# Attention weights of the last layer: block-diagonal tiles against dense tiles in pairs of 64 rows

## Chip, cores and metric

The kernel runs on one NeuronCore of a Trainium2 chip, in one launch. All data is float32. The metric is device time in microseconds (us). Three runs of the kernel before gave 1648.38, 1644.84 and 1645.3 us; the median is 1645.3 us.

## The reference, cut to what matters

128 sequences of 64 tokens with 128 channels go through four layers. Layers 0 to 2 are transformer blocks with 16 heads; the change does not touch what they compute. In layer 3 each sequence has a single-head attention over its own 64 context rows:

```
nx = layer_norm(x) * gamma + beta
q, k, v = nx @ Wq, ctx @ Wk, ctx @ Wv
weights = softmax(q k^T / sqrt(128))        # 64 x 64 for each sequence
evidence = weights @ v
combined = [nx, evidence, anchor]           # anchor: one vector per sequence
routed = sum over 3 experts of softmax(combined @ router_W) * (silu(combined @ e_w1) @ e_w2 + e_b2)
g = sigmoid(silu(combined @ gate_w1) @ gate_w2)
out = x + g * (routed @ out_w + out_b)
```

The kernel folds Wk into Wq, and Wv into the weights that evidence is multiplied by, so "evidence" in the kernel is softmax weights times raw context rows, called u.

## The kernel before, in words

The 8192 tokens are worked on in 16 groups (NST) of 512 tokens. A group is 8 sequences, held as four tiles (TT) of 128 rows, two sequences to a tile. Layers 0 to 2 alternate attention stages and MLP stages over the 16 groups. Layer 3 is the last stage, and it overlaps the end of the second MLP stage.

The order of every engine is written out by hand: pieces of work (small functions) are called one after the other, and each engine runs its instructions in the order of those calls. For layer 3 the list is `turn` (L1080): one turn does the hidden layers, the gate and the output of group a, and between them the attention pieces of groups a+1 and a+2. Turns 0 to 14 each hold one `turn_weights` and one `evidence`, for groups 1 to 15. Those of group 0 are called from `heads` (L1064), between the last turns of the MLP stage (L1199 to L1201); there `evidence` of group 0 follows directly on a `leave` of the MLP (L683: four transposes into the tile psB, which DVE then adds to x, L687).

The pieces that matter here, for one group:

- `load` (L897): one DMA from SP brings the context, tile c, 128 rows by 4 tiles by 128 channels (three buffers). `norm` (L903) loads the transposed context and lets POOL normalise x.
- `score` (L922): eight products of 64 columns give the scores psc (128 rows, 4 tiles, 64 keys), two sequences to a tile in the two halves of the rows. DVE subtracts the maximum.
- `weights` (L933): ACT takes the exponential, DVE the sum and its reciprocal. POOL then writes the shares into a tile pd of 128 rows by 4 tiles by 128 columns, in two instructions of 64 rows each (L943): sequence 0 of a tile into rows and columns 0 to 63, sequence 1 into rows and columns 64 to 127. The other half of pd is zero, set once by two memsets in `l3_loads` (L766).
- `turn_weights` (L947): four transposes of 128x128 (in the helper `transposed`, L317, so their line is L321) put pd's transpose into PSUM, and ACT copies 128x512 to pT (L950).
- `evidence` (L952): four products, context tile (128x128) as the stationary operand and 128 columns of pT as the moving one (L955). The zeros keep the two sequences apart. ACT copies 128x512 to u (L959).
- `router` (L961) and, in the next turn, `hidden` (L1005; L1013 and L1014) read u.

A float32 product is two instruction pairs on TensorE (a weight load and a matmul each); a transpose is one. So the four products of `evidence` are eight matmul records in the trace.

PSUM tiles of nx, queries, score, turn_weights, evidence and gate all come from the pool "mm" (L160), which has two buffers that are handed out in turn; a new tile waits for the readers of the tile that had its buffer.

Of the kernel before, what the change touches and what calls it, by code (L numbers as in the profile page):

```python
# [11 lines left out]
ALU = mybir.AluOpType  # L12
# [3 lines left out]
P = 128  # L16
NST = 16
TT = 4
NB = 8
L = 64  # L20
NT = TT * P
# [38 lines left out]
def tile_kernel(ctx: ExitStack, tc: tile.TileContext, a: dict, out: bass.AP):  # L60
    nc = tc.nc
    V, S, G, T = nc.vector, nc.scalar, nc.gpsimd, nc.tensor
# [3 lines left out]
    def const(shape, name):  # L66
        return cp.tile(shape, F32, tag=name, name=name)

    x_d = a["x"].rearrange("b n c -> (b n) c").rearrange("(s t p) c -> s p t c", t=TT, p=P)
    ctx_d = a["ctx_1024"].rearrange("b n c -> (b n) c").rearrange("(s t p) c -> s p t c", t=TT, p=P)  # L70
    out_d = out.rearrange("b n c -> (b n) c").rearrange("(s t p) c -> s p t c", t=TT, p=P)


# [32 lines left out]
    for name, n in (("L0_xcond_ca_proj_b", P), ("L1_xcond_bp", P), ("L2_xcond_b_cproj", P), ("L3_xcond_router_b", 3)):  # L106
        t = const([P, n], name)
# [10 lines left out]
    ident = const([P, P], "ident")  # L118
# [41 lines left out]
    def mm(name):  # L160
        return pools[1].tile([P, 512], F32, tag="mm", name=name)
# [150 lines left out]
    def stats_of(pool, src, eps):  # L312
        mv = pool.tile([P, TT, 2], F32, tag="mv", name="mv")
        stats(pool, src, mv)
        return mv, inv_std(pool, mv, eps)

    def transposed(psum, src):  # L317

        ps = psum.tile([P, 512], F32, tag="mm", name="psT")
        for t in range(TT):  # L320
            T.transpose(ps[:, ts(t, P)], src[:, t, :], ident)  # L321
        return ps
# [403 lines left out]
    def kept(shape, name, tag=None):  # L726
        return cp.tile(shape, F32, tag=tag or name, name=name)

    k3 = {}
    l3_pool = [None]  # L730

    def l3_loads():
        pool = l3_pool[0]
        e_w1 = a["L3_xcond_e_w1"].rearrange("e (k p) n -> p e k n", p=P)
        k3["w_1"] = kept([P, 3, 256], "w_1", "L0_xcond_adaln_w")
        k3["raw1"] = pool.tile([P, 6, 256], F32, tag="raw1", name="raw1", bufs=1)
        for ex in range(3):
            nc.sync.dma_start(k3["raw1"][:, 2 * ex : 2 * ex + 2], e_w1[:, ex, 1:3])
        k3["raw2"] = pool.tile([P, 6, P], F32, tag="raw2", name="raw2", bufs=1)
        nc.sync.dma_start(  # L740
            k3["raw2"], a["L3_xcond_e_w2"].rearrange("e (k p) n -> p (e k) n", p=P)
        )
        for ex in range(3):
            nc.sync.dma_start(k3["w_1"][:, ex], e_w1[:, ex, 0])
        r = _ROW["L3_xcond_gate_b2"]
        k3["g_b2"] = kept([P, P], "g_b2")
        nc.sync.dma_start(k3["g_b2"], a["vecs"][r : r + 1, :].broadcast_to([P, P]))
        r = _ROW["L3_xcond_out_b"]
        k3["out_b"] = kept([1, P], "out_b")
        nc.sync.dma_start(k3["out_b"], a["vecs"][r : r + 1, :])  # L750

        k3["r_b"] = kept([P, 1], "r_b")
        G.memset(k3["r_b"], 0.0)
        for t in range(TT):
            nc.sync.dma_start(
                k3["r_b"][32 * t : 32 * t + 3, :],
                a["L3_xcond_router_b"].rearrange("(n o) -> n o", o=1),
            )
        k3["one"] = kept([1, P], "one")
        G.memset(k3["one"], 1.0)  # L760
        k3["rw"] = kept([P, 3, 32], "rw")
        G.memset(k3["rw"], 0.0)
        k3["b_2o"] = kept([P, 3, P], "b_2o", "L0_xcond_fc1_w")
        for i in range(2):
            k3[f"pd{i}"] = kept([P, TT, P], f"pd{i}", ("L0_xcond_fc2_w", "L0_xcond_qkv_w")[i])
            G.memset(k3[f"pd{i}"], 0.0)  # L766
            k3[f"pr{i}"] = kept([P, TT, 3], f"pr{i}")
        k3["w_qk"] = kept([P, P], "w_qk")
        k3["w_gev"] = kept([P, P], "w_gev")
        k3["w_ev"] = kept([P, 3, 256], "w_ev", "L2_xcond_W_mod")  # L770
        k3["w_2o"] = kept([P, 6, P], "w_2o", "mod_L0_xcond_adaln_w")
        k3["ab"] = kept([P, 7, P], "ab")
        k3["ra"] = kept([P, NST, 2], "ra")
# [110 lines left out]
    def layer_3():  # L884

        pmm = pools[1]
# [6 lines left out]
        def sb(shape, tag, bufs=2):  # L893
            of = pools[0] if tag in shared else l3_pool[0]
            return of.tile(shape, F32, tag=shared.get(tag, tag), name=tag, bufs=bufs)

        def load(d):  # L897
            s = d["s"]
            d["c"] = sb([P, TT, P], "c", 3)
            nc.sync.dma_start(d["c"], ctx_d[s])  # L900
            d["mv"], d["rs"] = stats_of(l3_pool[0], xs[s], 1e-5)

        def norm(d):  # L903
# [29 lines left out]
        def weights(d):  # L933
            e = d["e"]
            S.activation(e, e, AF.Exp, scale=P ** -0.5)
            sm = sb([P, TT], "sm")
            V.tensor_reduce(sm, e, AX.X, ALU.add)
            V.reciprocal(sm, sm)

            pd = d["pd"] = k3["pd%d" % (d["s"] % 2)]  # L940
            for h in range(2):
                r = ts(h, L)
                G.tensor_tensor(  # L943
                    pd[r, :, r], e[r], sm[r].unsqueeze(2).broadcast_to([L, TT, L]), ALU.mult
                )

        def turn_weights(d):  # L947
            ps = transposed(pmm, d["pd"])
            d["pT"] = sb([P, NT], "pT")
            S.copy(d["pT"], ps)  # L950

        def evidence(d):  # L952
            ps = mm("pu")
            for t in range(TT):
                T.matmul(  # L955
                    ps[:, ts(t, P)], d["c"][:, t, :], d["pT"][:, ts(t, P)], start=True, stop=True
                )
            d["u"] = sb([P, NT], "u", 3)
            S.copy(d["u"], ps)  # L959

        def router(d):  # L961
            ps = small("pr")
# [97 lines left out]
        def go(f, j, *more):  # L1060
            if 0 <= j < NST:
                f(ds[j], *more)

        heads = [  # L1064
            lambda: (go(load, 0), go(load, 1)),
            lambda: go(norm, 0),
            lambda: (go(nx, 0), go(norm, 1)),
            lambda: (go(queries, 0), go(score, 0), go(load, 2)),
            lambda: (go(weights, 0), go(nx, 1), go(norm, 2)),
            lambda: (go(turn_weights, 0), go(queries, 1), go(score, 1)),  # L1070
            lambda: (go(evidence, 0), go(load, 3)),
        ]

        def bridge():
            go(router, 0)
            go(weights, 1)
            go(logits, 0)
            go(shares, 0)

        def turn(a_):  # L1080
            b_, c_ = a_ + 1, a_ + 2
            return [
                lambda: go(norm, c_ + 1),
                lambda: go(hidden, a_, 6),
                lambda: go(output, a_ - 1, 1),
                lambda: go(hidden, a_, 0),
                lambda: go(nx, c_),
                lambda: go(output, a_ - 1, 2),
                lambda: go(hidden, a_, 1),
                lambda: go(turn_weights, b_),  # L1090
                lambda: go(output, a_ - 1, 3),
                lambda: go(hidden, a_, 2),
                lambda: go(evidence, b_),
                lambda: go(load, c_ + 2),
                lambda: go(hidden, a_, 3),
                lambda: go(router, b_),
                lambda: go(hidden, a_, 4),
                lambda: go(biases, a_),
                lambda: go(queries, c_),
                lambda: go(hidden, a_, 5),  # L1100
                lambda: go(logits, b_),
                lambda: go(score, c_),
                lambda: go(gate, a_),
                lambda: go(output, a_, 0),
                lambda: go(shares, b_),
                lambda: go(weights, c_),
            ]
# [138 lines left out]
```

## Time and profile before

| | us |
|---|---|
| median of three runs | 1645.3 |
| profiled execution, own time | 1650.16 |
| its span, first to last instruction | 1648.4 |
| TensorE matmul (PE) busy over the span | 1590.4 |
| VectorE (DVE) busy | 1289.0 |
| GpSimd (POOL) busy | 1070.9 |
| ScalarE (ACT) busy | 1030.8 |
| TensorE clock granted, share of full | 0.996 |

The profile is of one execution. Its timeline lists instructions by start, with neighbours of one kind merged: start, duration, engine, line, operation, output<-inputs, for TensorE the part of the array used (rows*columns), the shape, and a count. The duration of a merged entry reaches to the end of its last instruction; since matmuls are pipelined, the next entry starts before that. PEld is the weight load that goes ahead of each matmul. A matmul's own duration holds the time it takes through the array, so the pace of the engine is read from start to start.

### The profile page before, as it was taken

How to read it: one execution, taken by the hardware profiler on the slowest of the kernel's cores; microseconds unless marked ns; L12 is line 12 of the kernel's file. 1: busy time of each engine (PE TensorE's matmuls, PEld its weight loads, DVE VectorE, ACT ScalarE, POOL GpSimd, SP SyncE). 2: the span in 40 equal slices, each digit the busy share in tenths (PEclk: the TensorE clock that was granted, in tenths of full speed). 3: DMA queues.
4: the chain of work that ended last, by engine and by line, in shares of the span. 5: the costliest groups of instructions: out<-in, count | busy, mean ns of one | idle time of the engine just before them, and what ended most of it. 6: DMA issues, size and time to landing. Idle time of an engine off the chain costs nothing.

```text
span 1648.4 us, 64206 instructions
## 1 busy us (share of the span) xinstructions
PE 1590.4 (96%) x27552; PEld 1066.6 (65%) x27552; DVE 1289.0 (78%) x2424; ACT 1030.8 (63%) x1696; POOL 1070.9 (65%) x1818
## 2 busy tenths in 40 slices
PE   6999999998999899999999999998999999999998
PEld 4677767776554467777776677776554566666665
DVE  6999989998576688899999999996453666666665
ACT  5878767776333677878878888885334444444442
POOL 5687777776899889987787776766654333334322
PEclk9999999999999999999999999999999999999999
DMA  7333443322202022212333432221200111111100
GB/s 206 81 93 86 105 119 91 89 79 61 60 27 60 21 60 62 66 47 55 86 94 85 107 85 73 62 60 43 79 1 7 35 34 36 39 33 39 30 14 17
DMA packets 137148, 104.15 MB, mean 63 GB/s; under 512 B 35045, under 2 KB 115615, under 8 KB 136863
## 3 DMA queue, kind: packets, MB, share of 16 engines
q1 hardware_dynamic: 136656, 100.01, 22.8%
q8 instruction: 217, 3.56, 0.9%
q14 instruction: 68, 0.56, 0.1%
q10 hardware_dynamic: 207, 0.03, 0.0%
HBM read 75.60 MB, written 13.89 MB: 54 GB/s over the span
## 4 chain that ended last, share of the span: by engine, by line
PE 78%; DVE 12%; ACT 3%; POOL 3%; DMA 2%; issue 2%; SPq 0%; POOLq 0%; DVEq 0%; ACTq 0%
PE sc L457 9%; PE pp L482 9%; PE po L499 7%; PE ph L1013 6%; PE ph L668 6%; PE ph L1014 6%; PE py L674 6%; PE psT L321 5%; PE po L1044 5%; DVE e L466 5%; DVE mx L464 5%; PE pk L415 4%; PE py L547 4%; PE pvv L438 3%; PE pq L428 3%
## 5 line engine op out<-in xcount | busy, mean ns | idle before, releaser
L486 ACT ACTIVATE eT<-pp 128x1024 f32<-128x1024 f32 x320 | 329.8, 1031 | 161.9 <-PE pp L482 161.9
L464 DVE TENSOR_REDUCE mx<-sc 128x32 f32<-128x2048 f32 x160 | 366.5, 2291 | 62.0 <-PE sc L457 62.0
L466 DVE TENSOR_TENSOR e<-sc,mx 128x2048 f32<-128x2048 f32 x160 | 366.6, 2291 | 5.5
L482 PEld LDWEIGHTS pp<-ident,e 64*128 64x128 f32 x5120 | 185.2, 140 | 142.4 <-ACT eT L486 45.2
L423 POOL TENSOR_SCALAR kbd<-kT,mask 128x512 f32<-128x512 f32 x316 | 213.2, 693 | 41.8 <-ACT kT L417 39.2
L482 PE MATMUL pp<-ident,e 64*128 64x64 f32 x5120 | 229.1, 230 | 8.4 <-DVE e L466 4.7
L351 POOL TENSOR_SCALAR xn<-x,nmu,rs 128x128 f32<-128x128 f32 x508 | 221.8, 451 | 13.3
L541 POOL TENSOR_TENSOR oT<-o,rb 128x512 f32<-128x512 f32 x80 | 102.1, 1276 | 154.3 <-DMA rb<-recs 71.3
L457 PE MATMUL sc<-kbd,qT 32*64 32x256 f32 x5120 | 181.0, 390 | 15.7 <-DVE e L466 14.6
L669 ACT ACTIVATE h<-ph,vec 128x512 f32<-128x512 f32 x128 | 87.4, 688 | 158.4 <-PE ph L668 158.3
L499 PE MATMUL po<-eT,vbd 128*32 128x64 f32 x10240 | 179.9, 222 | 1.6 <-issue 1.4
L1020 ACT ACTIVATE h<-h 128x512 f32<-128x512 f32 x112 | 69.1, 628 | 160.4 <-DVE h L1016 132.6
L499 PEld LDWEIGHTS po<-eT,vbd 128*32 128x32 f32 x10240 | 152.7, 110 | 15.1 <-issue 2.5
L309 POOL TENSOR_TENSOR rs<-rs,nhalf 128x4 f32<-128x4 f32 x128 | 130.4, 1018 | 10.7
L457 PEld LDWEIGHTS sc<-kbd,qT 32*64 32x64 f32 x5120 | 97.9, 132 | 52.8 <-issue 19.5
L1016 DVE TENSOR_TENSOR h<-ph,ab 128x512 f32<-128x512 f32 x112 | 76.9, 687 | 64.5 <-PE ph L1014 64.3
L299 DVE BATCH_NORM_STATS2 st<-x 128x6 f32<-128x128 f32 x512 | 110.4, 278 | 1.4 <-DMA x<-in_x_dram 0.8
L1037 POOL TENSOR_SCALAR g<-g 128x512 f32<-128x512 f32 x16 | 10.0, 625 | 140.4 <-ACT g L1036 140.4
L1013 PE MATMUL ph<-nx,w 128*128 128x512 f32 x192 | 99.8, 601 | 0.0
L507 ACT COPY o<-po 128x512 f32<-128x512 f32 x160 | 95.8, 598 | 5.8 <-PE po L499 3.3
L1044 PEld LDWEIGHTS po<-w_2o,h 128*128 128x128 f32 x768 | 92.2, 192 | 10.9 <-issue 8.4
L1049 DVE SCALAR_TENSOR_TENSOR acc<-po,pr,acc 128x128 f32<-128x128 f32 x192 | 67.2, 350 | 40.1 <-PE po L1044 35.6
(256 smaller groups left out, 2904.9 us busy)
## 6 DMA issues: line engine op xcount, KB each, us to landing
rb<-recs SPq DMA_DIRECT2D x80, 256.0 KB
c<-in_ctx_dram SPq DMA_DIRECT2D x80, 256.0 KB
o<-o SPq DMA_DIRECT2D x320, 32.0 KB
gt<-gate_L_xcond_sa_proj_w SPq DMA_DIRECT2D x32, 256.0 KB
gt<-gate_L_xcond_W_proj SPq DMA_DIRECT2D x32, 256.0 KB
x<-in_x_dram SPq DMA_DIRECT2D x16, 256.0 KB
ctxT<-cm SPq DMA_DIRECT2D x16, 256.0 KB
cT<-ctxT SPq DMA_DIRECT2D x16, 256.0 KB
```

The source lines that it names most:

```text
L299: V.bn_stats(st[:, t, :], src[:, t, :])
L309: G.tensor_tensor(rs, rs, nhalf, ALU.pow)
L351: engine.tensor_scalar(xn[:, t, :], src[:, t, :], nmu[:, t : t + 1], rs[:, t : t + 1], ALU.add, ALU.mult)
L423: (V if at.get("first") else G).tensor_scalar(kbd[:, j], by_batch(kT), mask[:, j : j + 1], 1.0, ALU.mult, ALU.mult)
L457: T.matmul(sc[ts(h, L), g, ts(t2, 256)], qT[ts(g, 32), ts(b, L)], kbd[ts(g, 32), :, b, :], start=True, stop=True,)
L464: V.tensor_reduce(mx, sc.rearrange("p g (m k) -> p (g m) k", k=L), AX.X, ALU.max)
L466: V.tensor_tensor(e, sc.rearrange("p g (m k) -> p (g m) k", k=L), mx.unsqueeze(2).broadcast_to([P, 32, L]), ALU.subtract,)
L482: T.transpose(pp[:, h, ts(4 * g2 + 2 * i + t2, L)], e6[ts(h, L), 2 * gg + g2, t2, i], ident[ts(h, L), ts(h, L)],)
L486: S.activation(eT[:, gg], pp, AF.Exp, scale=HD ** -0.5)
L499: T.matmul(po[ts(g, 32), i, ts(2 * t2 + h, L)], at["vbd"][:, 4 * u + 2 * t2 + h, 2 * g + i, :], e7[:, g // 2, h, g % 2, i, t2, :], start=T ...
L1013: T.matmul(ps, wn, d["nx"], start=True, stop=False)
L1044: T.matmul(po[:, ex, :], d[q][:, ts(t, P)], k3["w_2o"][:, q, :], start=r == 0, stop=r == 1)
```

## The change

The diff keeps the softmax shares dense. POOL writes one tile pn of 128 rows by 4 tiles by 64 keys in one instruction, and the zero-filled tiles and their memsets go. `turn_weights` transposes two tiles of 64 keys side by side as one 128x128 transpose, so there are two transposes for a group, and ACT copies 128x256. In the transpose, rows 0 to 63 hold the keys of the first tile of a pair and rows 64 to 127 those of the second (r = 0, 1); the columns hold the two sequences of a tile (h = 0, 1). `evidence` becomes eight products of 64 rows, 64x128 stationary and 64 columns moving, r = 0 and r = 1 in turn, on the upper and lower half of the array's rows. The two halves write to two PSUM tiles of the pool mm, and two ACT copies of 128x2x128 put them in order into u. The context is loaded to suit, with four DMAs of 64 rows by 2 sequences by 128 channels in place of one.

```diff
+    ctx_pairs = a["ctx_1024"].rearrange("(s i r h) k c -> s i r k h c", i=2, r=2, h=2)
...
         for i in range(2):
-            k3[f"pd{i}"] = kept([P, TT, P], f"pd{i}", ("L0_xcond_fc2_w", "L0_xcond_qkv_w")[i])
-            G.memset(k3[f"pd{i}"], 0.0)
             k3[f"pr{i}"] = kept([P, TT, 3], f"pr{i}")
...
         def load(d):
             s = d["s"]
-            d["c"] = sb([P, TT, P], "c", 3)
-            nc.sync.dma_start(d["c"], ctx_d[s])
+            d["c"] = sb([P, 4, P], "c", 3)
+            for i in range(2):
+                for r in range(2):
+                    nc.sync.dma_start(d["c"][ts(r, L), ts(i, 2), :], ctx_pairs[s, i, r])
...
-            pd = d["pd"] = k3["pd%d" % (d["s"] % 2)]
-            for h in range(2):
-                r = ts(h, L)
-                G.tensor_tensor(
-                    pd[r, :, r], e[r], sm[r].unsqueeze(2).broadcast_to([L, TT, L]), ALU.mult
+            d["pn"] = sb([P, TT, L], "pn")
+            G.tensor_tensor(
+                d["pn"], e, sm.unsqueeze(2).broadcast_to([P, TT, L]), ALU.mult
+            )
...
         def turn_weights(d):
-            ps = transposed(pmm, d["pd"])
-            d["pT"] = sb([P, NT], "pT")
-            S.copy(d["pT"], ps)
+            ps = mm("psT")
+            for i in range(2):
+                T.transpose(
+                    ps[:, ts(i, P)], d["pn"][:, ts(i, 2), :].rearrange("p t k -> p (t k)"), ident
                 )
+            d["pT"] = sb([P, 2, 2, L], "pT")
+            S.copy(d["pT"].rearrange("p i h q -> p (i h q)"), ps[:, 0 : 2 * P])
...
         def evidence(d):
-            ps = mm("pu")
-            for t in range(TT):
-                T.matmul(
-                    ps[:, ts(t, P)], d["c"][:, t, :], d["pT"][:, ts(t, P)], start=True, stop=True
-                )
+            ps = [mm("pu") for r in range(2)]
+            for i in range(2):
+                for h in range(2):
+                    for r in range(2):
+                        T.matmul(
+                            ps[r][:, ts(2 * i + h, L)], d["c"][ts(r, L), 2 * i + h, :],
+                            d["pT"][ts(r, L), i, h, :], start=True, stop=True,
+                        )
             d["u"] = sb([P, NT], "u", 3)
-            S.copy(d["u"], ps)
+            u4 = d["u"].rearrange("p (i r c) -> p r i c", i=2, r=2)
+            for r in range(2):
+                S.copy(u4[:, r], ps[r][:, 0 : 2 * P].rearrange("p (i c) -> p i c", i=2))
```

More of the change, by code (lines that the diff above doesn't have):

```diff
@@ L938, in weights, with turn_weights @@
             V.reciprocal(sm, sm)
-            pd = d["pd"] = k3["pd%d" % (d["s"] % 2)]
-            for h in range(2):
-                r = ts(h, L)
-                G.tensor_tensor(
-                    pd[r, :, r], e[r], sm[r].unsqueeze(2).broadcast_to([L, TT, L]), ALU.mult
-                )
-        def turn_weights(d):
-            ps = transposed(pmm, d["pd"])
-            d["pT"] = sb([P, NT], "pT")
-            S.copy(d["pT"], ps)
+            d["pn"] = sb([P, TT, L], "pn")
+            G.tensor_tensor(
+                d["pn"], e, sm.unsqueeze(2).broadcast_to([P, TT, L]), ALU.mult
+            )
+        def turn_weights(d):
+            ps = mm("psT")
+            for i in range(2):
+                T.transpose(
+                    ps[:, ts(i, P)], d["pn"][:, ts(i, 2), :].rearrange("p t k -> p (t k)"), ident
+                )
+            d["pT"] = sb([P, 2, 2, L], "pT")
+            S.copy(d["pT"].rearrange("p i h q -> p (i h q)"), ps[:, 0 : 2 * P])
         def evidence(d):
-            ps = mm("pu")
-            for t in range(TT):
-                T.matmul(
-                    ps[:, ts(t, P)], d["c"][:, t, :], d["pT"][:, ts(t, P)], start=True, stop=True
-                )
+            ps = [mm("pu") for r in range(2)]
[6 more added lines that the diff above has]
+                        )
             d["u"] = sb([P, NT], "u", 3)
-            S.copy(d["u"], ps)
+            u4 = d["u"].rearrange("p (i r c) -> p r i c", i=2, r=2)
+            for r in range(2):
+                S.copy(u4[:, r], ps[r][:, 0 : 2 * P].rearrange("p (i c) -> p i c", i=2))
         def router(d):
```

## Prediction

> **What bounds the kernel now.** I read the page's busy line first, then busy time by stretches, then the timeline of TensorE and the weight-load rows by shape. Over the whole span:
>
> ```profile
> PE 1590.4 (96%) x27552; PEld 1066.6 (65%) x27552; DVE 1289.0 (78%) x2424; ACT 1030.8 (63%) x1696; POOL 1070.9 (65%) x1818
> ```
>
> That is an average over stages; the change touches only the last. From turn 0 of layer 3 to the last turn, one stretch holds nearly all of it:
>
> ```profile
> 1286.00:1618.00 332.00, 332.00 (x1967) 212.08 (x1966) 216.69 (x647) 147.37 (x233) 116.62 (x245) 1.00 0.11 31
> ```
>
> PE (first pair) is busy 332.00 of 332.00 us at a granted clock of 1.00; DVE 216.69, ACT 147.37 and POOL 116.62 have room. So here only what PE's own instructions take counts, and what another engine gives back is worth nothing. One turn's pieces, on PE:
>
> ```profile
> 1312.27 0.60 PE L321 MATMUL psT<-ident,pd 128*128 128x128 f32 x4
> 1312.70 1.50 PE L1044 MATMUL po<-w_2o,h 128*128 128x128 f32 x12
> ...
> 1315.76 1.05 PE L955 MATMUL pu<-pT,c 128*128 128x128 f32 x8
> 1316.65 0.59 PE L1013 MATMUL ph<-nx,w 128*128 128x512 f32 x1
> ```
>
> From start to start, the four transposes take 1312.70 - 1312.27 = 0.43 us and the evidence 1316.65 - 1315.76 = 0.89 us: 0.111 us for each of eight records of 128 columns.
>
> **The transposes.** Two go of four, same shape, same part of the array, no new neighbours: 0.43 / 2 = 0.22 us saved for a group.
>
> **The evidence.** Sixteen records take the place of eight: for each half of the array's rows four products of two passes, each with a load of 64x128 and 64 moving columns. The moving columns halve. The load does not, and what a load takes is in these rows (mean ns last before the bar's end):
>
> ```profile
> L965 PEld LDWEIGHTS pr<-u,rw 128*32 128x32 f32 x120 | 3.6, 110 | 0.0
> L927 PEld LDWEIGHTS psc<-cT,qT 128*64 128x64 f32 x240 | 8.2, 137 | 8.3 <-issue 6.8 <-ACT qT L920 1.5
> L955 PEld LDWEIGHTS pu<-pT,c 128*128 128x128 f32 x120 | 15.6, 191 | 6.8 <-issue 6.2 <-ACT pT L950 0.6
> L482 PEld LDWEIGHTS pp<-ident,e 64*128 64x128 f32 x3456 | 125.0, 140 | 94.0 <-ACT eT L486 33.5 <-ACT vbd L444 19.6 <-issue 15.5
> ```
>
> 110, 137 and 191 ns for 32, 64 and 128 columns: 0.84 ns a column (54 / 64). A transpose's load (L482) has 128 columns and takes 140, as much as 64 columns of a product. So the transposes pp, which have the new evidence's very form (64 rows, 128 columns loaded, 64 moved, halves in turn), load twice as fast as it will. That a product waits for its load when few columns move is seen where 3 columns move:
>
> ```profile
> 1200.88 0.30 PEld L798 LDWEIGHTS ps<-L_xcond_router_W,wT 128*128 128x128 f32 x2
> 1201.11 0.73 PEld L811 LDWEIGHTS ps<-raw,wT 128*128 128x128 f32 x4
> ```
>
> Two loads take 1201.11 - 1200.88 = 0.23 us though the products between them move 3 columns: 0.112 each. The other question is whether the halves run side by side. Eight pairs of pp, eight pairs of psc (column halves), and what surrounds them:
>
> ```profile
> 601.40 0.59 PE L428 MATMUL pq<-xm,L_xcond_Wq 128*128 128x512 f32 x1
> 601.92 0.71 PE L482 MATMUL pp<-ident,e 64*128 64x64 f32 x16
> 602.57 1.15 PE L438 MATMUL pvv<-L_xcond_Wkv,cm 128*64 128x64 f32 x32
> ...
> 1323.44 0.27 PE L977 MATMUL pl<-ident,lgT 128*128 128x128 f32 x1
> 1323.64 0.69 PE L927 MATMUL psc<-cT,qT 128*64 128x64 f32 x16
> 1324.26 0.38 PE L1026 MATMUL pg<-L_xcond_gate_w,h 128*128 128x128 f32 x1
> ```
>
> They do: sixteen records of pp in 0.65 us; in narrow windows of the timeline two start within 3 to 7 ns and a pair follows the last by 0.062 us (pp) or 0.058 us (psc), about what 64 moved columns take (64 x 0.84 = 54 ns).
>
> No row has a product of 64 rows in this form. **Its pace is bounded** from below by pp's 0.062 us a pair, from above by two loads one after the other, 2 x 0.112 = 0.224. I take 0.115, the load of 128 columns at 0.112 plus the few ns by which the second half trails, because the load rows say which of two things ends last. Then, for one group:
> - entering the other division of the array: pq's last 512 columns start at 601.40 and take 0.43, pp starts at 601.92: 0.09;
> - first to last pair: the first load is not hidden, so the first step is 0.21 (load and load), then 6 x 0.115 = 0.69: 0.90;
> - last start to the next form's load: 0.15 (pp's last start at 602.41 to pvv);
> - that form's first product shows its whole load: pg's first record 0.38 against its usual 0.275: 0.10.
>
> Together 1.24 to 1.25 us against 0.89: 0.36 lost for a group. The nearest row agrees in kind: the two one-row products L843 (1*128, 128 columns loaded) stand from 1228.06 to 1228.47 between products L838 that start at 1227.74: 0.10 late in (2 x 0.112 would be 1227.96), and 0.41 for what takes 0.22 undivided.
>
> The Trainium skill, in "TensorEngine Tiling (Array Packing)", section "Theoretical Speedup", promises up to 2x where the contraction is 64 or less. By that rule the evidence would fall to 0.45 us and, with the transposes, 15 groups would save 9.9 us. The trace's load rows stand against it, so the sum does not use it.
>
> Net for groups 1 to 15: 15 x (0.36 - 0.22) = +2.2 us.
>
> **Group 0** lies between MLP turns. There a second thing happens: evidence now takes both buffers of the pool mm, and one was just given to psB.
>
> ```profile
> 1277.96 0.60 PE L686 MATMUL psB<-ident,y 128*128 128x128 f32 x4
> 1278.39 1.06 PE L955 MATMUL pu<-pT,c 128*128 128x128 f32 x8
> 1279.29 1.02 PE L674 MATMUL py<-h,L_xcond_W_mlp 128*128 128x512 f32 x2
> ...
> 1278.16 0.75 DVE L678 SCALAR_TENSOR_TENSOR y<-py,vec,mod_L_xcond_W_mod 128x512 f32<-128x512 f32 x1 [6.17 <-PE py L674]
> 1278.83 0.68 DVE L687 TENSOR_TENSOR x<-x,psB 128x512 f32<-128x512 f32 x1
> ```
>
> The built program shows a wait on DVE at the second evidence product: it must wait until L687 has read psB, at 1278.83 + 0.68 = 1279.51. PE runs in order, so the last MLP products (py) and all behind them wait too. Evidence's second half starts at 1279.56 and py at 1279.56 + 0.90 + 0.15 + 0.10 = 1280.71, not 1279.29: +1.4 us. What follows on PE, DVE (y, the router's logits) and ACT hangs on py and shifts with it. The 0.22 us saved in group 0's transposes is lost: the next product (pq, 1268.57) sat 0.56 us waiting for DVE's L687 anyway.
>
> **Costed at nothing**, with the cover:
> - POOL: two writes of 0.65 us become one (between 0.6 and 1.3), 3.4 us before their reader (1308.88 to 1312.27); the memsets (0.98 us at 1178.58) lie where PE has 40.0 us of 40 busy.
> - ACT: pT's copy shrinks (0.57 to about 0.4, as the exponential of 128x256 takes); u needs two of about 0.4 for one of 0.57, so u comes 0.2 us later after evidence. It was ready at 1317.79 and first read by the router's second half at 1318.71: 0.9 us. Beyond that, each 0.1 would cost 15 x 0.1.
> - SP: four DMA issues of 0.42 for one, 1.3 us more, in front of a cT load 7.4 us later (1316.95, 1324.37) and the outputs; context is loaded three turns (68 us) ahead, and its bytes and 512 B rows stay.
> - The pool mm serves seven tiles a turn, not six. In a steady turn each buffer's reader is done over 1 us before: pq takes the first half of u's (copied by about 1318), psc the second, pg pq's (copied 1322.90, needed 1324.26).
>
> **Sum:** +2.2 + 1.4 = +3.6 us. The profiled execution took 1650.16 us (span 1648.4), 4.9 over the median, so a like profile would show 1653.8; from the median 1645.3 the forecast is 1648.9 us.
>
> **Rivals.**
> 1. Loads keep up, pp's pace: 0.09 + 0.49 + 0.15 + 0.10 = 0.84 against 0.89. A group saves 0.05 + 0.22 = 0.27, fifteen 4.1; group 0 loses 1.0. Net -3.1: 1642.2 us, not slower. For it: pp has this form. Against: its load is 140 ns, a product's 191. A group breaks even at a pace of 0.093 us a pair (0.34 + 0.21 + 6 x 0.093 = 0.89 + 0.22), the whole, with group 0's stall, at about 0.08.
> 2. The halves do not run side by side: 16 x 0.112 + 0.35 = 2.14, +1.25 a group; less 0.22, fifteen give +15.5, group 0 +2.3: 1663.1 us. Against: pp and psc.
> 3. Evidence as forecast, but no stall at group 0 (its cost 0.36): +2.2 + 0.4: 1647.9 us, within the bound. Against: the wait in the program and DVE's end at 1279.51.
>
> **Chances.** Forecast 0.70, rival 1 0.10, rival 2 0.07, rival 3 0.13. About 0.2%, 3.3 us, can be told from no change. The forecast lies just over it: 0.45 of its 0.70 slower, 0.25 the same. With rival 2 slower is 0.52; with rival 3 and 0.03 of rival 1 the same is 0.41; faster 0.07. The range leaves rivals 1 and 2 out (0.17): 1645.0 to 1653.0, for a pace of 0.112 to 0.14 a pair, some 0.05 in either switch, and runs that spread over 3.5 us.
>
> **What would show it.** Weight loads of pu at about 190 ns in the form 64*128, pairs 0.112 to 0.118 us apart, 1.25 us from pu's first start less 0.09 to the next steady product; psT of pn 0.22 us; pu waiting on DVE once, about 1.1 us, near 1278; a turn of 22.6 us (the router's transpose pl recurs every 22.59) grown by 0.14. Loads of 140 ns would make rival 1 right; a wait of the router on ACT in every turn, or of pu on SP's DMA, would make the sum wrong.

## The result and the profile after

In 18 runs each, the kernel before takes 1647.87 us (median) and the changed one 1651.81 us. The ratio over these runs is 1.0022, 95% interval 1.0015 to 1.0029: 3.6 us slower, between 2.5 and 4.8 (the two medians differ by 3.9). The profiled execution of the changed kernel took 1652.54 us, with a span of 1650.7.

The busy line of the page after, and the stretch of layer 3 that the prediction showed of before, moved by 0.53 us to begin at the same work (start:end and length; busy time and records of PE, PEld, DVE, ACT, POOL; granted clock; DMA share; GB/s):

```profile
PE 1592.1 (96%) x27648; PEld 1063.5 (64%) x27648; DVE 1288.0 (78%) x2424; ACT 1028.1 (62%) x1712; POOL 1056.3 (64%) x1800
```

```profile
1286.53:1618.53 332.00, 332.00 (x2041) 207.01 (x2041) 214.61 (x642) 145.09 (x248) 107.06 (x230) 1.00 0.11 31
```

PE is still busy all the time in this stretch, at full clock. DVE, ACT and POOL show 2.1, 2.3 and 9.6 us less busy time in it, and that bought nothing. So PE's turns, and group 0 ahead of them, answer for the time. The router's transpose pl comes once a turn; here are its records in before, then in the changed kernel (count; shortest, middle and longest in ns; first and last start):

```profile
L977 PE MATMUL pl<-ident,lgT x14: 273/273/273, 1300.8 to 1594.6; 128*128 128x128 f32 x14
```

```profile
L989 PE MATMUL pl<-ident,lgT x13: 272/272/273, 1301.5 to 1574.1; 128*128 128x128 f32 x13
```

Before: 293.8 us for 13 turns, 22.60; after: 272.6 for 12 turns, 22.72. By the single records it is 22.593 and 22.717, each of these turns like the last within 1 ns: 0.124 us more. One turn of the changed kernel on PE (start, duration, engine, line, operation, output<-inputs, part of the array, shape, count):

```profile
1312.90 0.38 PE L951 MATMUL psT<-ident,pn 128*128 128x128 f32 x2
1313.12 1.50 PE L1056 MATMUL po<-w_2o,h 128*128 128x128 f32 x12
...
1316.27 1.11 PE L964 MATMUL pu<-pT,c 64*128 64x64 f32 x16
1317.31 1.12 PE L1025 MATMUL ph<-nx,w 128*128 128x512 f32 x2
```

Two transposes take 0.22 us from start to start (four took 0.43), and evidence 1317.31 - 1316.27 = 1.04 us (0.89 before). The rest of its loss is not between these two starts: pu starts 0.09 later after the product ahead of it, and the product behind it is 0.10 longer (1.12 for two records; a steady pair has 1.02). The loads of pu, by shape (busy us, mean ns of one, idle before):

```profile
L964 PEld LDWEIGHTS pu<-pT,c 64*128 64x128 f32 x256 | 15.8, 187 | 12.3 <-issue 10.8 <-DVE x L688 0.8 <-ACT pT L955 0.8
```

187 ns against 191 for the load of 128 rows: half the rows, nearly the same time. And group 0, with the stall on DVE (the idle time and its releaser stand in brackets), then the addition that ends it:

```profile
1277.09 0.60 PE L687 MATMUL psB<-ident,y 128*128 128x128 f32 x4
1277.62 0.43 PE L964 MATMUL pu<-pT,c 64*128 64x64 f32 x2
1278.69 1.10 PE L964 MATMUL pu<-pT,c 64*128 64x64 f32 x14 [0.64 <-DVE x L688]
1279.72 3.70 PE L675 MATMUL py<-h,L_xcond_W_mlp 128*128 128x512 f32 x8
...
1277.96 0.68 DVE L688 TENSOR_TENSOR x<-x,psB 128x512 f32<-128x512 f32 x1
```

The first half's product runs at 1277.62, the second half's only when L688 has read psB (1277.96 + 0.68 = 1278.64).

Executions start layer 3 up to 4 us apart, so I compare each trace from one place: the sixth psB from the end (1248.63 in before, 1248.08 after) to the start of the last record. That is 399.69 us before and 402.60 after: +2.91. The terms: -0.32 up to pq of group 1, +1.40 from there to the first pl, +0.10 in the first turn, 14 x 0.124 = +1.74 in the others; before rounding they add up to 2.91.

### The profile page after: what moved, and what is told of

It reads as the page before. It is cut to its first block, busy times and chain, and to the rows that moved or that the text cites. A ratio compares the mean times of both kernels' runs of the same rounds, so it can differ in the third digit from the quotient of the medians.

```text
span 1650.7 us, 64458 instructions
## 1 busy us (share of the span) xinstructions
PE 1592.1 (96%) x27648; PEld 1063.5 (64%) x27648; DVE 1288.0 (78%) x2424; ACT 1028.1 (62%) x1712; POOL 1056.3 (64%) x1800
## 4 chain that ended last, share of the span: by engine, by line
PE 79%; DVE 13%; ACT 3%; POOL 2%; issue 1%; DMA 1%; SPq 0%; POOLq 0%; DVEq 0%; ACTq 0%
PE sc L458 9%; PE pp L483 9%; PE po L500 7%; PE ph L1025 6%; PE ph L1026 6%; PE ph L669 5%; DVE e L467 5%; DVE mx L465 5%; PE py L675 5%; PE po L1056 5%; PE psT L322 5%; PE pk L416 5%; PE py L548 4%; PE pvv L439 3%; PE pq L429 3%; ACT cm L339 1%
## 5 line engine op out<-in xcount | busy, mean ns | idle before, releaser
L1056 PE MATMUL po<-w_2o,h 128*128 128x128 f32 x768 | 96.4, 275 | 1.8 <-ACT h L1032 1.8
```

Of the source, the lines that this page charges most:

```text
L1056: T.matmul(po[:, ex, :], d[q][:, ts(t, P)], k3["w_2o"][:, q, :], start=r == 0, stop=r == 1)
```

## Experiments

Theory: evidence in 64-row halves is paced by the weight load of 128 columns, which the halving does not shorten, and pays for entering and leaving the divided array; at group 0 it waits for a buffer of mm. Rivals: the moved columns or the number of records set the pace; the halves take turns; the four loads or the copies on ACT cost the time. All runs in one table (the turn is pl to pl; "trace" is from that psB to the last record, less 399.69; "timed" is the ratio to before, which was run again beside each set, with its interval, and the same in us; where a kernel has one run, its trace alone is used):

| kernel | turn, us | trace, us | timed |
|---|---|---|---|
| before | 22.593 | 0 | |
| changed | 22.717 | +2.91 | 1.0022 [1.0015, 1.0029], +3.6 |
| e1 zeros after | 22.375 | -2.77 | 0.9990 [0.9981, 0.9999], -1.6 |
| e2 first earlier | 22.717 | +1.85 | 1.0012 [1.0003, 1.0020], +2.0 |
| e3 twice moved | 22.771 | +3.78 | one run |
| e4 one half | 22.711 | +1.75 | one run |
| e5 half by half | 23.212 | +10.82 | one run |
| e6 quarters | 22.304 | -3.70 | 0.9984 [0.9975, 0.9993], -2.6 |
| e7 quarters, earlier | 22.304 | -4.76 | 0.9965 [0.9952, 0.9977], -5.8 |
| e8 four loads | 22.593 | 0.00 | 0.9999 [0.9988, 1.0011], -0.2 |
| e9 quarters, twice moved | 22.713 | +2.84 | one run |

### e1: the transposes alone

The two tiles pd0 and pd1 (128 x 4 x 128) and their memsets come back as the place of pT. Of evidence only the new lines are shown; they take the place of the eight half products and the two copies.

```diff
-            d["pT"] = sb([P, 2, 2, L], "pT")
-            S.copy(d["pT"].rearrange("p i h q -> p (i h q)"), ps[:, 0 : 2 * P])
+            d["pT"] = k3["pd%d" % (d["s"] % 2)]
+            for r in range(2):
+                S.copy(
+                    d["pT"][ts(r, L), :, ts(r, L)],
+                    ps[ts(r, L), 0 : 2 * P].rearrange("p (t q) -> p t q", t=TT),
+                )
...
+            ps = mm("pu")
+            p4 = ps.rearrange("p (i r h q) -> p i r h q", i=2, r=2, h=2)
+            for t in range(TT):
+                T.matmul(
+                    p4[:, t // 2, :, t % 2, :], d["c"][:, t, :], d["pT"][:, t, :],
+                    start=True, stop=True,
+                )
...
+            S.copy(d["u"], ps)
```

> The zeros come back, but only where the products read them: POOL writes pn dense and two transposes turn it, as in the changed kernel, and ACT's copy puts the turned weights into a block diagonal (two copies of 64 partitions into a tile whose zeros were written once). Evidence is again four products over all 128 rows with 128 moved columns, into one buffer of mm, with one copy of u. The four context loads stay. Theory (the loss is the evidence's 64-row form, paced by its weight loads, and the wait for the second buffer at group 0): evidence 0.89 us again, the router's transpose pl recurs every 22.593 - 0.218 = 22.375 us, no wait on DVE in group 0, and in all 15 x 0.218 plus the 0.32 of group 0's transposes = 3.6 us less than before (ratio 0.9978). Rival 1 (the loss is in the four context loads or in the changed order of mm's buffers): the turn stays at 22.6 to 22.7. Rival 2 (ACT's two copies of pT are late): products pu wait on ACT in every turn and the turn shrinks less than 0.1.

The turn is 22.375, to the nanosecond as expected: two transposes fewer are worth 0.218 us, and all that the changed kernel loses in a turn lies in the evidence. The whole came to -2.77 in the trace, not -3.6. PE's rows of e1 show where the two copies of pT (0.76 us for the pair) are late after all:

```profile
1265.33 1.13 PE L922 MATMUL pq<-nx,w_qk 128*128 128x512 f32 x2 [0.90 <-ACT pd L958]
...
1290.00 1.16 PE L969 MATMUL pu<-pd,c 128*128 128x128 f32 x8 [0.16 <-ACT pd L958]
```

At group 0 pq waits 0.90 us for that copy (the changed kernel: 0.46), and the first turn, which has no output products between the transposes and evidence, shows 0.16 us of idle time there. Against the forecast the first place costs 0.44 us and the first turn 0.39, together the 0.83 that is missing. Rival 2 as it was put, with waits in every turn, is out: the lateness shows at these two places alone.

### e2: group 0's evidence earlier

The call moves into turn 15 of the second MLP, behind the second output product.

```diff
             go(enter, j + 1)
+            if mv_out is None and j in early:
+                early[j]()
...
+    early = {}
...
-            lambda: (go(evidence, 0), go(load, 3)),
+            lambda: go(load, 3),
...
+        early[NST - 1] = lambda: go(evidence, 0)
```

> The changed kernel with group 0's evidence issued inside the last full MLP turn, right after the second output product, and not after that turn's transposes psB; all else as it was. Theory: group 0 lost 1.41 us, of which 0.34 is the 64-row form and 1.07 the wait for the buffer that psB holds. Here the wait on DVE is gone from pu's records, the turn stays at 22.717, and the time is 1.07 us under the changed kernel's, that is 2.5 us over before (ratio 1.0015). Rival (the stall only moves: u's two copies push ACT's Gelus, or psB waits for u's copy): as much idle time on PE appears at the MLP's products or at psB, and the time stays at +3.6 us (1.0022).

PE's rows of e2 where evidence stands now, and where it stood:

```profile
1270.97 1.11 PE L967 MATMUL pu<-pT,c 64*128 64x64 f32 x16
1272.01 1.12 PE L669 MATMUL ph<-xm,L_xcond_W_mlp 128*128 128x512 f32 x2
...
1275.55 0.60 PE L687 MATMUL psB<-ident,y 128*128 128x128 f32 x4
1275.99 3.60 PE L675 MATMUL py<-h,L_xcond_W_mlp 128*128 128x512 f32 x8
```

No wait is left and none has come up elsewhere; from that psB on the trace is 402.60 - 401.54 = 1.06 us shorter than the changed kernel's. The stall was the buffer's, and its price is shown.

### e3: twice the moved columns

```diff
-                            ps[r][:, ts(2 * i + h, L)], d["c"][ts(r, L), 2 * i + h, :],
-                            d["pT"][ts(r, L), i, h, :], start=True, stop=True,
+                            ps[r][:, ts(2 * i + h, P)], d["c"][ts(r, L), 2 * i + h, :],
+                            d["pT"][ts(r, L), i, :, :], start=True, stop=True,
...
```

> The changed kernel with twice the moved columns: each product moves the weights of both h (128 columns), and ACT copies only the half that counts. Loads, records and halves as they were. Theory (the load of 128 columns sets the pace): pairs of pu records stay 0.112 to 0.12 us apart, the block within 0.1 us of 1.23, the turn 22.72 to 22.82. Rival (moved columns set the pace, 64 of them at the 0.112 seen): pairs 0.22 us apart, the block 0.9 us longer, the turn 23.6.

PE's rows in the timeline of e3:

```profile
1314.34 1.16 PE L964 MATMUL pu<-pT,c 64*128 64x128 f32 x16
1315.44 1.12 PE L1028 MATMUL ph<-nx,w 128*128 128x512 f32 x2
```

By the single records these starts are 1.092 us apart, 0.054 more than with half the moved columns, and the turn is 22.771, longer by as much. Pairs stay 0.112 us apart; only the first step grows, from 0.160 to 0.213. Beside a load of 128 columns, the moved columns do not set the pace.

### e4: one half of the products

```diff
-            ps = [mm("pu") for r in range(2)]
+            ps = [mm("pu")] * 2
...
-                    for r in range(2):
+                    for r in range(1):
```

> The changed kernel without the products of the lower 64 rows (r = 1): eight records of pu in place of sixteen, one buffer of mm; the half of u that they gave is filled from the upper rows' products, so that part of the output is not computed. Theory (the halves run side by side, each paced by its own load): records 0.112 us apart, the block shorter by under 0.05 us, the turn 22.67 to 22.72; at group 0 no wait for the second buffer, 1.07 us less. Rival (the halves take turns, each taking half of the 0.112): records 0.056 apart, the block 0.4 us shorter, the turn 22.3.

PE's rows in the timeline of e4:

```profile
1313.93 1.10 PE L964 MATMUL pu<-pT,c 64*128 64x64 f32 x8
1314.97 0.70 PE L1025 MATMUL ph<-nx,w 128*128 128x512 f32 x1
```

Half the records take the same 1.04 us; the turn is 6 ns shorter. The two halves run wholly side by side, so the second half is free, and each record of the first takes as long as one of the whole product did (0.112 us).

### e5: one half after the other

```diff
-            for i in range(2):
-                for h in range(2):
-                    for r in range(2):
+            for r in range(2):
+                for i in range(2):
+                    for h in range(2):
```

> The changed kernel with the loop over the halves outermost: the four products of the upper rows first, then the four of the lower rows; the same sixteen records, loads and buffers. Theory (records are issued in order, so a half only works beside the other where their records alternate): 16 records 0.112 us apart except one overlap at the change of half, the block about 0.75 us longer, the turn 23.4 to 23.5. Rival (each half has a queue of its own and runs ahead): pairs as before, the turn 22.72.

PE's rows in the timeline of e5:

```profile
1315.96 1.60 PE L964 MATMUL pu<-pT,c 64*128 64x64 f32 x16
1317.49 1.12 PE L1025 MATMUL ph<-nx,w 128*128 128x512 f32 x2
```

1.53 us, and a turn of 23.212: between the two expectations, and neither is right. In the single records the lower half's first record, known by its 0.320 us (a half's first takes 0.320, its others 0.272), starts 6 ns after the upper half's fifth, and then both run side by side until the upper half is done. So records are not strictly held to their order; the other half runs ahead, but only by about three records of eight. That the halves alternate is worth 0.49 us a turn.

### e6: quarters

```diff
-                        T.matmul(
-                            ps[r][:, ts(2 * i + h, L)], d["c"][ts(r, L), 2 * i + h, :],
-                            d["pT"][ts(r, L), i, h, :], start=True, stop=True,
-                        )
+                        for c in range(2):
+                            T.matmul(
+                                ps[r][ts(c, L), ts(2 * i + h, L)],
+                                d["c"][ts(r, L), 2 * i + h, ts(c, L)],
+                                d["pT"][ts(r, L), i, h, :], start=True, stop=True,
+                            )
```

> The changed kernel with each evidence product split once more, by output channels: 64 rows by 64 columns of the array, 32 records in place of 16, each loading 64 columns and moving 64. Theory (the pace is the weight load, 0.84 ns for each loaded column, and the parts of the array load side by side): loads of about 140 ns in place of 187, four records start every 0.06 us, the block shrinks from 1.23 us to about 0.09 + 0.11 + 6 x 0.06 + 0.20 + 0.10 = 0.86, the turn to about 22.35, and the time to 16 x 0.37 = 5.9 us under the changed kernel's, 2.3 under before (ratio 0.9986). Rival 1 (the number of records sets the pace, 0.056 us each as now): 32 x 0.056, the block grows to 2.1 us, the turn to 23.6 and the time by 14 us over the changed kernel's. Rival 2 (column parts load one after the other): pace 0.112 for four records, nothing changes: turn 22.717, ratio 1.0022.

PE's rows of e6, then its loads:

```profile
1316.36 0.69 PE L965 MATMUL pu<-pT,c 64*64 64x64 f32 x32
1316.99 1.12 PE L1027 MATMUL ph<-nx,w 128*128 128x512 f32 x2
```

```profile
L965 PEld LDWEIGHTS pu<-pT,c 64*64 64x64 f32 x512 | 9.1, 134 | 12.4 <-issue 10.8 <-DVE x L688 0.9 <-ACT pT L955 0.8
```

Twice the records, and 0.63 us in place of 1.04. A load takes 134 ns, not 187; four records start within 20 ns, and the next four 0.058 us later. The turn is 22.304, 0.41 under the changed kernel's and 0.29 under before's. Both rivals fall, and this carries the theory: halving the loaded columns halves the time from one set of records to the next, which neither halving the records (e4) nor doubling the moved columns (e3) touched. Quarters also halve the width of each part of the array, but width alone is not the cause: the transposes pp, in parts of 64*128 with loads of 140 ns, follow at 0.062 us. The expected block of 0.86 us was 0.04 too long, on the way out (below).

### e7: quarters, and group 0 earlier

The edits of e2 and e6 together.

> The quarters (64 rows by 64 columns of the array) and group 0's evidence issued earlier, in one kernel. Theory (the two edits act in different places and add up): the turn 22.304 as with quarters, no wait on DVE at group 0, 1.06 us less than the quarters alone: about 3.7 to 4.8 us under before (ratio 0.9971 to 0.9978). Rival (the stall at group 0 only gives way to the next wait once evidence is short): the time stays that of the quarters, ratio 0.9984.

PE's rows in the timeline of e7:

```profile
1274.74 0.69 PE L968 MATMUL pu<-pT,c 64*64 64x64 f32 x32
1275.37 1.12 PE L669 MATMUL ph<-xm,L_xcond_W_mlp 128*128 128x512 f32 x2
...
1279.34 3.60 PE L675 MATMUL py<-h,L_xcond_W_mlp 128*128 128x512 f32 x8
```

No wait; 395.99 - 394.93 = 1.06 us less than the quarters alone: the edits add up. At 0.9965 [0.9952, 0.9977] of before this version beats both kernels; in the traces it is 4.76 us under before and 7.67 under the changed kernel.

### e8: the four loads alone

```diff
-            nc.sync.dma_start(d["c"], ctx_d[s])
+            for i in range(2):
+                for r in range(2):
+                    nc.sync.dma_start(
+                        d["c"][ts(r, L), ts(i, 2), :], ctx_d[s][ts(r, L), ts(i, 2), :]
+                    )
```

> The kernel before with one part of the change alone: each group's context comes in four transfers of the changed kernel's shape (64 partitions, two tiles), with before's order of rows; all else is before. Theory (SP and the queues have room): the turn stays 22.593, and the time is before's, ratio 1.0000 within its interval. Rival (the measured times of the four kernels timed so far lie 0.7 to 1.2 us above what their traces' sums from the end of the MLP give, and the transfers are the cause): ratio 1.0005, with waits on SP's DMA or a longer stretch around the first loads at 1238 to 1290.

The trace agrees with before's within 0.01 us over 400 us, and the time is before's. The loads cost nothing; the changed order of rows, which e8 leaves out, is in e1, whose turn came as expected. So the spread between traces and timed runs is not theirs. It is also smaller than the expectation says: for e2 it is 0.2 us, and every timed interval holds its trace's sum.

### e9: quarters with twice the moved columns

e3's edit on e6.

> The quarters with twice the moved columns: each product moves the weights of both h (128 columns, 0.107 us by the runs so far), its load stays at 64 columns; ACT copies only the half that counts. Theory (a part's pace is the larger of its load and its moved columns, the first step is their sum, and the way out depends on the columns loaded): four records start every 0.107 to 0.112 us, first step 0.16, the way out 0.15 as with quarters; first to last record 0.16 + 6 x 0.107 + 0.02 = 0.82 us, the turn 22.304 + 0.82 - 0.477 = 22.65. Rival (the pace is the load alone, in quarters as in halves): four every 0.058, the turn under 22.37. Rival 2 (load and moved columns never overlap within a part): four every 0.16, the turn 22.98.

PE's rows in the timeline of e9:

```profile
1313.76 1.10 PE L965 MATMUL pu<-pT,c 64*64 64x128 f32 x32
1314.80 1.13 PE L1030 MATMUL ph<-nx,w 128*128 128x512 f32 x2
```

1.04 us again: with loads of 64 columns, 128 moved columns set the pace, four records every 0.109 us. So the load alone is not the rule either; the larger of the two is. The turn is 22.713, 0.06 more than expected: 0.05 of it on the way out, which the expectation took to go by the loaded columns.

Four kernels now give the parts of the block, from their single records (us; "out" is from the last record's start to the next product's start):

| loaded, moved columns | first step | pace | out |
|---|---|---|---|
| 128, 64 (changed) | 0.160 | 0.112 | 0.202 |
| 128, 128 (e3) | 0.213 | 0.112 | 0.202 |
| 64, 64 (e6) | 0.107 | 0.058 | 0.149 |
| 64, 128 (e9) | 0.160 | 0.109 | 0.199 |

At 0.84 ns a column (54 ns for 64, 107 for 128): the first step is load and moved columns one after the other, the pace is the larger of the two, and the way out is one more pace and 0.09.

## Why the prediction was right, and where it was not

- **The bound.** PE's own instructions, right: 332.00 of 332.00 us busy again, and lighter DVE, ACT and POOL were worth nothing.
- **Transposes.** 0.22 us a group; e1 alone shows 0.218.
- **The pace.** 0.115 us a pair was taken, from the load of 128 columns; 0.112 came, and e3, e4, e6 and e9, with pp beside them, show that the load of 128 columns is its cause. Rival 1 (pp's pace, 0.062) failed for the reason given: the load. Rival 2 (no overlap) is excluded by e4.
- **The block.** Of its four terms, entry (0.09) and the next form's load (0.10) were right. First to last pair was 0.84, not 0.90: the first step holds one load and 64 moved columns (0.160), not two loads (0.21), and the pace was 3 ns quicker. The way out was 0.20, not 0.15: pp's 0.15 holds pp's own pace of 0.062, and with a pace of 0.112 it is 0.20. The two errors nearly cancel: +0.342 a group against the forecast's 0.36. So the net for a turn is 0.124, not 0.14 to 0.15, and for groups 1 to 15 +1.8, not +2.2.
- **Group 0's stall.** +1.40 us measured, 1.4 forecast; e2 puts 1.06 of it on the buffer. Rival 3 (no stall) is out. "PE runs in order" was enough here, since the products behind the waiting one did wait; between two halves it is not strict, as e5 shows.
- **The step that failed:** "The 0.22 us saved in group 0's transposes is lost". PE gained 0.32 there. The prediction let pq of group 1 wait for L687, as before. In the changed kernel pq waits for ACT's copy of pT instead:

```profile
1267.70 1.13 PE L920 MATMUL pq<-nx,w_qk 128*128 128x512 f32 x2 [0.46 <-ACT pT L955]
```

  The two readers of that moment, on ACT and DVE:

```profile
1267.28 0.37 ACT L955 COPY pT<-psT 128x256 f32<-128x256 f32 x1 [0.82 <-PE psT L951]
1267.29 0.68 DVE L688 TENSOR_TENSOR x<-x,psB 128x512 f32<-128x512 f32 x1
```

  The copy ends at 1267.65, and pq starts at 1267.70, while DVE reads psB until 1267.97. So pq has psT's buffer here, not psB's as before. The front part says that mm's buffers are handed out in turn; this row does not fit that. What made the choice differ was not tried.
- **Costed at nothing.** POOL's one write, the four loads (e8) and u's two copies cost nothing. The four issues take SP 2.56 us from the first's start to the last's end, where four of 0.42 were reckoned; it still has room.
- **The sum.** With its parts as the traces measure them the forecast would have been +2.9, not +3.6. The timed +3.6 (2.5 to 4.8) holds both; 0.7 us can't be told apart here. That forecast and measurement agree to a tenth is partly luck; the two main terms were right.
- **The time itself.** The forecast of 1648.9 us stood on a median of three runs, 1645.3. Over 18 runs that median is 1647.87, so the changed kernel's 1651.81 lies 2.9 us over the forecast, though inside its range of 1645.0 to 1653.0. Only the difference was forecast well.

In "TensorE: Matmul & The Clock Gate", section "LDWEIGHTS (loading the stationary operand)", the Trainium skill says that a load's time goes by its columns and not by the rows it is summed over, columns / 1.2 in ns. By that formula an estimate is 107 ns for 128 columns and 53 for 64. The runs agree within 5 ns, with paces of 112 and 58 ns where the load decides; the loads' own bars in the profile are longer, 187 and 134 ns. The "up to 2x" of "TensorEngine Tiling (Array Packing)", section "Theoretical Speedup", for a contraction of 64 did not come: the halves run side by side (e4), but each of their records takes as long as one of the whole. In this case a gain came only with the cut by columns as well: from the first to the last record 0.78 us before, 0.84 in halves, 0.48 in quarters (e6).

## What to carry to other kernels

Before a product is cut by rows to save zeros, price its weight load: each part goes at the pace of the larger of loaded and moved columns, and cutting rows shortens neither, so cut the loaded columns too where both are small. Add the price of the division for each block (here 0.09 us in, 0.09 and one pace out, 0.10 on the next product), which this block in halves did not earn back. And when a step takes a second buffer of a pool, look at who holds it in each place where the step stands, not only in the steady turn; moving one call was worth 1.06 us (e2).

## What the runs showed of the hardware that was not expected

- The way out of a divided block depends on its pace (0.149 us at 0.058, 0.20 at 0.11): in these four kernels it is one pace and a fixed 0.09, not a fixed whole.
- All four quarters load side by side: four loads of 64 columns in 0.058 us (e6), the pace that two column halves have in psc.
- One part of the array runs ahead of the order of records by about three records when its own turn comes later (e5).
